# 120 instead of 116 single-row tiles in a two-layer graph convolution: the spacing of the tiles that SyncE and ScalarE fetch row by row

## The chip, the cores and the metric

The kernel runs on one core of a Trainium2 chip. Of the core's engines, TensorE (PE) multiplies, VectorE (DVE) and ScalarE (ACT) work element by element, GpSimd (POOL) issues the gathers with computed row numbers, and SyncE (SP) and ScalarE also issue plain DMAs from queues of their own. The metric is the device time of one execution in microseconds. The median of three runs of the kernel before is 3784.03 us (3783.49 to 3790.35).

## The reference

12500 nodes of 128 features, 200000 edges sorted by destination, 8 relations (edge types). Two layers of the same form run one after the other, then a layer norm. Cut to what matters:

```python
for l in range(2):
    W = einsum('rb,bio->rio', comp[l], basis[l])       # one 128x128 matrix per relation
    xw = einsum('ni,rio->nro', h, W)
    msgs = xw[src, et]                                 # one row per edge: the gather
    summed = segment_sum(msgs, dst * 8 + et)           # per node and relation
    mean = summed / max(count, 1)
    agg = mean.reshape(N, 8, 128).sum(axis=1)
    h = relu(agg + h @ root[l] + bias[l]) + h
out = layernorm(x + h)
```

## The kernel before

The edges lie in 1563 tiles of 128 edges. For each tile the 128 source rows (512 bytes each) must come into SBUF, where a matmul with a one-hot matrix (`dm`, written by VectorE, the weight of each edge in it) sums them by destination. Eight tiles make a quad, 196 quads in all (the last has three tiles); quad q holds tiles 8q to 8q+7.

Layer 1 gathers rows of `x` (12500 rows) and multiplies by the relation matrices after the sum (`means`, `take_means`, `product`, `place`). At its end it writes a table `y_d` of 8 x 12500 rows, each node's features times each relation's matrix. Layer 2 gathers rows of `y_d` and needs only the one-hot matmuls (`add_rows`), a bias, the root matrix and the layer norm (`norm`, in 13 groups of about 1024 nodes).

**How a tile's rows come in.** Nearly all tiles are gathered by GpSimd: `gather(l, q)` issues one indirect DMA of 128 rows for each tile of the quad (line 766) into a ring of seven quad buffers (`rows`), so the gather of quad q+7 needs TensorE to be done with quad q. For the last six quads (190 to 195) the gather of quad q also waits until TensorE is done with quad q-3 (`after = [("done", l)]`). The other tiles are the "single-row" tiles. Lists say which:

```python
# engine, first tile, end, every so many, rows per chunk, quads of lead, host buffers
("SP", 62, 1552, 49, 32, 15, [... 4 hosts in sT ...])
```

Every so many tiles, one tile is left out of GpSimd's work. Its 128 rows are fetched by 128 plain DMAs of one row each, issued by SyncE or ScalarE (`lone_rows`, line 702), in chunks of 32 (16 on ScalarE in layer 1). Ahead of each chunk the engine loads the chunk's row addresses into registers (line 697). A chunk is put into the engine's program 15 quads (10 on ScalarE in layer 1) before the tile's quad, on ScalarE at most one chunk a quad. The rows land in a host buffer that is free at that time, three or four hosts in turn.

**What else is in those queues.** The order of each engine's work is written out once, in program order, by a planner (`Plan`) that adds only the waits that data needs. SyncE also loads `x` for the layer norm (`load_x`) and stores the result. ScalarE has most PSUM evacuations in layer 1. In layer 2 it has, beside its chunks, one square root for each norm group (`root_of`, line 1533); VectorE takes its reciprocal (`one_by`, line 1537) three quads later in program order, ahead of the one-hot matrices of the quads that follow (line 1188). The square root of group n stands at quad 22 + 16n of ScalarE's program, so for n = 10 at quad 182, behind every chunk whose quad of issue comes earlier.

**Between the layers.** GpSimd goes on with quads 0 and 1 of layer 2 while the end of layer 1 is worked off. Before quad 2 it issues one extra gather (line 760) that reads rows which only the last stores of `y_d` bring.

The single-row tiles before: layer 1, SyncE 32 (every 47th from 90), ScalarE 5 and 18 (every 64th); layer 2, SyncE 31 (every 49th from 62), ScalarE 30 (every 50th from 65). 55 + 61 = 116.

Of the kernel before, what the change touches and what calls it, by code (L numbers as in the profile page):

```python
# [8 lines left out]
F32 = mybir.dt.float32  # L9
# [419 lines left out]
def ordered_path(  # L429
# [68 lines left out]
    def keep(shape, dtype, name):  # L498
        return const.tile(shape, dtype, name=name)
# [16 lines left out]
    jmp = keep([P, P], I32, "jmp")  # L516
# [37 lines left out]
    comp_sb = keep([P, L * R * NB], F32, "comp_sb")  # L554
# [84 lines left out]
    def floats(t, n):  # L639
        return t[:, n * P:(n + 1) * P]  # L640

    sT_f = [t.rearrange("p r g k -> p (r g k)") for t in sT_r.tiles]
# [2 lines left out]
    mixer_f = mixer.rearrange("p m k -> p (m k)")  # L645
    idx_f = idx.bitcast(F32)
    lists = [
        [("SP", 90, 1552, 47, 32, 15, [(jmp.bitcast(F32), ["jmp"], []), (comp_sb, ["comp"], []),
                                     (sel.rearrange("p g k -> p (g k)"), ["sel"], [])]),
         ("ACT", 13 * Q + 2, 46 * Q, 8 * Q, 16, 10, [(floats(yr_f, j), yr_cells, yr_cells) for j in range(5)]),  # L650
         ("ACT", 53 * Q + 2, 1552, 8 * Q, 16, 10, [(floats(mixer_f, j), ["mixer"], []) for j in range(2)])],
        [("SP", 62, 1552, 49, 32, 15, [(floats(sT_f[0], j), [("sT", 0, 0), ("sT", 0, 1)], []) for j in range(4)]),
         ("ACT", 65, 1552, 50, 32, 15, [(floats(sT_f[1], j), [("sT", 1, 0), ("sT", 1, 1)], []) for j in range(4)])]]
    single, at_row = [{}, {}], [0, 0]
    for l in range(L):
        for k, (_, t0, t1, by, _, _, hosts) in enumerate(lists[l]):
# [513 lines left out]
    dms, sT, ys, pl, ym = {}, {}, {}, {}, {}  # L1170
# [646 lines left out]
def kernel(  # L1817
# [18 lines left out]
    flag = ctx.enter_context(tc.tile_pool(name="flag", bufs=1))  # L1836
    bad = flag.tile([1, 1], I32, name="bad")
    plan = ordered_path(tc, bad, x, src, dst, et, basis, comp, root, bias, out)
    every = [mybir.EngineType.PE, mybir.EngineType.Activation, mybir.EngineType.DVE, mybir.EngineType.Pool,
             mybir.EngineType.SP]  # L1840
# [36 lines left out]
```

## Time and profile before

| | |
|---|---|
| median of three runs | 3784.03 us |
| the profiled execution's own time | 3783.55 us |
| its span, first to last instruction | 3781.7 us |
| GpSimd busy | 2844.7 us (75%), 3019 instructions |
| TensorE busy | 2413.2 us (64%) |
| VectorE busy | 1694.7 us (45%) |
| ScalarE busy | 354.0 us (9%) |

In the profile, an instruction's row has its start, its duration, the engine, the line, the operation, and in brackets the idle time of the engine before it with what ended it. Issues of DMAs have the engine's name with a q (SPq, ACTq) and count in no busy time: a queue that is full of single-row DMAs reads as idle in the table above. For GpSimd, the 0.3 us between two gathers stand as idle time ended by "issue", which means that nothing seen in the profile was waited for.

### The profile page before, as it was taken

To read this page: it belongs to the slowest core of one execution; us is meant where nothing else is said; L and a number is where in the kernel's file an instruction comes from. 1 tells how busy PE (TensorE), PEld (TensorE's weight loads), DVE (VectorE), ACT (ScalarE), POOL (GpSimd) and SP (SyncE) were. 2 spreads that over 40 slices of the span, in tenths; PEclk is the share of its full clock that TensorE was granted. 3 is DMA by queue.
4 is the path that set the end of the run, shared out by engine and by line. 5 is a ranking of instruction groups with operands and counts; after the bars stand their busy time and mean duration, and the time that the engine had idled before them with its cause. 6 is when DMAs were issued, how large, how long until landed. Compare 5 with 4: busy or idle time off the path is not lost.

```text
span 3781.7 us, 62930 instructions
## 1 busy us (share of the span) xinstructions
PE 2413.2 (64%) x11367; PEld 1933.4 (51%) x11367; DVE 1694.7 (45%) x4752; ACT 354.0 (9%) x794; POOL 2844.7 (75%) x3019
## 2 busy tenths in 40 slices
PE   5777667777666676777765555556566555655655
PEld 3566645555555555665543444444444444444444
DVE  5556424444333333343344444444444444454444
ACT  1121211211111111111100000000000000000000
POOL 7777777777777777777777777777777777777776
PEclk8999879999888888788888787777777777787778
DMA  4122223433322222223232222222222222222222
GB/s 125 56 62 62 56 92 102 123 111 101 99 87 81 89 89 84 84 82 96 92 85 55 56 62 61 65 63 61 66 56 67 66 56 67 60 62 67 67 54 61
DMA packets 155888, 286.71 MB, mean 76 GB/s; under 512 B 67013, under 2 KB 89474, under 8 KB 155482
## 3 DMA queue, kind: packets, MB, share of 16 engines
q0 software_dynamic: 96352, 197.52, 20.3%
q10 hardware_dynamic: 30461, 55.51, 4.5%
q1 hardware_dynamic: 28669, 29.60, 3.0%
q14 instruction: 314, 2.57, 0.2%
q8 instruction: 92, 1.51, 0.2%
HBM read 223.72 MB, written 58.65 MB: 75 GB/s over the span
## 4 chain that ended last, share of the span: by engine, by line
POOL 52%; issue 19%; DMA 11%; PE 9%; ACTq 4%; ACT 2%; DVE 2%; SPq 2%; POOLq 0%; DVEq 0%
POOL rows L766 52%; DMA rows<-y_d,idy 9%; ACTq L702 3%; PE s L1276 2%; PE s L1451 1%; SPq L702 1%; ACT sT L623 1%; ACTq L697 1%; PE y L1308 1%; DVE dm L1188 1%; PE pt L1406 1%; PE ct L959 1%; PE ct L960 1%; DVE arena L949 1%; PE pt L907 1%
## 5 line engine op out<-in xcount | busy, mean ns | idle before, releaser
L766 POOL DMA_INDIRECT rows<-in_x_dram,idx x1508 | 1425.2, 945 | 462.4 <-issue 455.7
L766 POOL DMA_INDIRECT rows<-y_d,idy x1502 | 1417.4, 944 | 458.5 <-issue 446.9
L1188 DVE TENSOR_SCALAR dm<-cols,near,w 128x256 f32<-128x256 f16 x1563 | 723.8, 534 | 952.1 <-PE s L1451 570.3
L1451 PE MATMUL s<-dm,rows 128*128 128x256 f32 x1984 | 659.9, 495 | 447.7 <-DMA rows<-y_d,idy 349.0
L1451 PEld LDWEIGHTS s<-dm,rows 128*128 128x128 f32 x1984 | 491.9, 257 | 580.2 <-issue 316.9
L1188 DVE TENSOR_SCALAR dm<-cols,kr,w 128x128 f32<-128x128 f16 x1563 | 524.9, 400 | 201.8 <-PE s L1276 177.5
L1276 PEld LDWEIGHTS s<-dm,rows 128*128 128x128 f32 x3016 | 436.3, 225 | 291.7 <-DMA rows<-in_x_dram,idx 243.0
L1276 PE MATMUL s<-dm,rows 128*128 128x128 f32 x3016 | 462.1, 313 | 189.0 <-DMA rows<-in_x_dram,idx 182.3
L1451 PE MATMUL ct<-dm,rows 128*128 128x256 f32 x1014 | 341.9, 501 | 294.2 <-DMA rows<-y_d,idy 281.4
L1451 PEld LDWEIGHTS ct<-dm,rows 128*128 128x128 f32 x1014 | 255.3, 262 | 364.2 <-issue 234.5
L1308 PE MATMUL y<-w_sb,sT 128*128 128x128 f32 x1968 | 270.1, 296 | 55.8 <-ACT sT L623 55.8
L1308 PEld LDWEIGHTS y<-w_sb,sT 128*128 128x128 f32 x1968 | 257.0, 211 | 64.6 <-ACT sT L623 63.6
L1406 PE MATMUL pt<-w_sb,arena 128*128 128x512 f32 (+1 forms) x386 | 222.5, 660 | 62.3 <-DVE y_row L626 42.3
L1339 PE MATMUL po<-pl,ys 128*128 128x256 f32 x392 | 138.4, 437 | 140.8 <-ACT sT L623 135.9
L623 ACT ACTIVATE sT<-s 128x512 f32<-128x512 f32 x391 | 213.5, 606 | 83.7 <-PE s L1276 83.4
L626 DVE COPY y_row<-pt 128x512 f32<-128x512 f32 x56 | 38.7, 691 | 364.6 <-PE pt L1406 364.6
L623 ACT ACTIVATE y_row<-pt 128x512 f32<-128x512 f32 (+1 forms) x139 | 83.0, 597 | 1041.7 <-PE s L1276 574.3
L1308 PE MATMUL ct<-w_sb,sT 128*128 128x128 f32 (+1 forms) x1168 | 159.8, 296 | 0.7 <-ACT sT L623 0.7
L1308 PEld LDWEIGHTS ct<-w_sb,sT 128*128 128x128 f32 (+1 forms) x1168 | 155.0, 213 | 1.3 <-ACT sT L623 1.1
L1533 ACT ACTIVATE st<-st,eps 128x8 f32<-128x8 f32 (+1 forms) x13 | 4.0, 308 | 1586.5 <-DMA sT<-y_d 736.9
L1339 PEld LDWEIGHTS po<-pl,ys 128*128 128x128 f32 x392 | 65.2, 201 | 169.0 <-ACT sT L623 159.0
L1360 DVE TENSOR_TENSOR po<-po,carry 128x128 f32<-128x128 f32 x98 | 29.0, 296 | 263.8 <-PE s L1276 242.7
(210 smaller groups left out, 1296.9 us busy)
## 6 DMA issues: line engine op xcount, KB each, us to landing
sT<-y_d SPq DMA_DIRECT2D x3968, 0.5 KB
sT<-y_d ACTq DMA_DIRECT2D x3840, 0.5 KB
y_d<-y_row ACTq DMA_DIRECT2D x96, 512.0 KB
mixer<-in_x_dram ACTq DMA_DIRECT2D x2304, 0.5 KB
rows<-in_x_dram,idx POOLq DMA_INDIRECT x1508
rows<-y_d,idy POOLq DMA_INDIRECT x1502
jmp<-in_x_dram SPq DMA_DIRECT2D x1408, 0.5 KB
comp_sb<-in_x_dram SPq DMA_DIRECT2D x1408, 0.5 KB
```

The source lines that it names most:

```text
L623: act(lambda: nc.scalar.activation(out_t, in_t, AF.Copy), reads, writes)
L626: vec(lambda: nc.vector.tensor_copy(out_t, in_t), reads, writes)
L697: _, at = nc.values_load_multi_w_load_instructions(offs[r:r + 1, l * P + j * ch:l * P + (j + 1) * ch], engines=[mybir.EngineType.SP if e = ...
L702: return [eng.dma_start(o[j * ch + i:j * ch + i + 1, :].bitcast(byte), table_b[bass.ds(v, 4 * D)].rearrange("(p d) -> p d", p=1)) for i, v ...
L766: ins.append(nc.gpsimd.indirect_dma_start(out=t[:, i - q * Q, :], out_offset=None, in_=table_t, in_offset=bass.IndirectOffsetOnAxis(ap=ids ...
L907: last = nc.tensor.matmul(pt[:, b, :], t[:, b, :], m, start=(i == 0), stop=(i == len(parts) - 1))
L1188: emits.append(lambda i=i: nc.vector.tensor_scalar(t[:, i - q * Q, :wide], cols[:, :wide], ids[:, i:i + 1], w[:, i:i + 1], op0=ALU.is_equa ...
L1276: last = nc.tensor.matmul(s_b[i // 4][0][:, i % 4, :], lones[i][0] if i in lones else t[:, i, :], d[:, i, :], start=True, stop=True)
L1308: last = nc.tensor.matmul(y[:m], t[:, r, :nt, :].rearrange("p t k -> p (t k)"), w_sb[:, 0, r, :], start=(r == 0), stop=(r == R - 1))
L1339: ins = nc.tensor.matmul(a, o[:m], t[:m], start=opens, stop=last and not root_in)
L1406: pe(lambda: nc.tensor.matmul(hb[:n].rearrange("p r d -> p (r d)"), hT[:, j * P:j * P + n], w_sb[:, 1, k * H:(k + 1) * H, :].rearrange("p ...
L1451: ins = nc.tensor.matmul(a, lones[i][0] if i in lones else t[:, i, :], d[:, i, :], start=(opens and i == 0), stop=(last and i == n - 1 and ...
```

## The change

```diff
-        [("SP", 90, 1552, 47, 32, 15, [(jmp.bitcast(F32), ["jmp"], []), (comp_sb, ["comp"], []),
+        [("SP", 91, 1552, 45, 32, 15, [(jmp.bitcast(F32), ["jmp"], []), (comp_sb, ["comp"], []),
                                      (sel.rearrange("p g k -> p (g k)"), ["sel"], [])]),
          ("ACT", 13 * Q + 2, 46 * Q, 8 * Q, 16, 10, ...),
          ("ACT", 53 * Q + 2, 1552, 8 * Q, 16, 10, ...)],
-        [("SP", 62, 1552, 49, 32, 15, [(floats(sT_f[0], j), ...) for j in range(4)]),
-         ("ACT", 65, 1552, 50, 32, 15, [(floats(sT_f[1], j), ...) for j in range(4)])]]
+        [("SP", 62, 1552, 47, 32, 15, [(floats(sT_f[0], j), ...) for j in range(4)]),
+         ("ACT", 63, 1552, 48, 32, 15, [(floats(sT_f[1], j), ...) for j in range(4)])]]
```

Three of the five lists get another spacing and two another first tile. Layer 1, SyncE: 33 tiles (91 to 1531) for 32 (90 to 1547). Layer 2, SyncE: 32 tiles (62 to 1519) for 31 (62 to 1532). Layer 2, ScalarE: 32 tiles (63 to 1551) for 30 (65 to 1515). 56 + 64 = 120. GpSimd issues 1 gather fewer in layer 1 and 3 fewer in layer 2; SyncE issues 256 more single-row DMAs and ScalarE 256 more. Every tile still has its one-hot matrix and its matmul; only the buffer that the matmul reads differs. The small loads that bring the row addresses of the tiles carry a few rows more each.

More of the change, by code (lines that the diff above doesn't have):

```diff
@@ L651, in ordered_path @@
          ("ACT", 53 * Q + 2, 1552, 8 * Q, 16, 10, [(floats(mixer_f, j), ["mixer"], []) for j in range(2)])],
-        [("SP", 62, 1552, 49, 32, 15, [(floats(sT_f[0], j), [("sT", 0, 0), ("sT", 0, 1)], []) for j in range(4)]),
-         ("ACT", 65, 1552, 50, 32, 15, [(floats(sT_f[1], j), [("sT", 1, 0), ("sT", 1, 1)], []) for j in range(4)])]]
+        [("SP", 62, 1552, 47, 32, 15, [(floats(sT_f[0], j), [("sT", 0, 0), ("sT", 0, 1)], []) for j in range(4)]),
+         ("ACT", 63, 1552, 48, 32, 15, [(floats(sT_f[1], j), [("sT", 1, 0), ("sT", 1, 1)], []) for j in range(4)])]]
     single, at_row = [{}, {}], [0, 0]
```

## The prediction

> **What bounds the kernel now.** I read the chain that ended last first, then the costliest groups, then GpSimd alone by stretches of time.
>
> ```profile
> span 3781.7 us, 62930 instructions
> POOL 52%; issue 19%; DMA 11%; PE 9%; ACTq 4%; ACT 2%; DVE 2%; SPq 2%; POOLq 0%; DVEq 0%
> L766 POOL DMA_INDIRECT rows<-in_x_dram,idx x1508 | 1425.2, 945 | 462.4 <-issue 455.7
> L766 POOL DMA_INDIRECT rows<-y_d,idy x1502 | 1417.4, 944 | 458.5 <-issue 446.9
> ```
> ```profile
> 2000.00:2100.00 100.00, 75.56 (x81) 0.80 0.25 56
> 2700.00:2800.00 100.00, 75.50 (x81) 0.69 0.27 61
> 3640.00:3740.00 100.00, 75.62 (x81) 0.80 0.20 60
> ```
>
> The second fence is GpSimd's gathers in three stretches of layer 2. A gather costs its busy time and the idle time before it: (1425.2 + 462.4) / 1508 = 1.252 us in layer 1, (1417.4 + 458.5) / 1502 = 1.249 us in layer 2. Nearly all of the idle time ends by "issue", so nothing is waited for; 1508 and 1502 gathers make 1887.6 + 1875.9 = 3763.5 of 3781.7 us. The pace is the same 81 per 100 us whether SyncE and ScalarE send single rows (first two stretches) or have stopped (the third). The kernel is GpSimd's row of gathers, with one real wait in it, between the layers:
>
> ```profile
> 1890.16 0.95 POOL L766 DMA_INDIRECT rows<-y_d,idy  x1 [0.30 <-issue]
> 1908.87 0.94 POOL L766 DMA_INDIRECT rows<-y_d,idy  x1 [0.30 <-issue]
> 1912.13 0.94 POOL L760 DMA_INDIRECT jmp<-y_d,fix_i  x1 [2.31 <-DMA y_d<-y_row]
> ```
> ```profile
> 1866.45 2.46 DMA rows<-in_x_dram,idx
> 1868.95 3.78 PE s L1276 x16
> ...
> 1907.31 4.08 DMA y_d<-y_row
> ```
>
> Layer 2's first 16 gathers run from 1890.16; the 17th (line 760) waits 2.31 us, 2.0 more than the usual 0.30. The chain (second fence) says for what: the rows of quad 192 land at 1868.9, TensorE works from there nearly without a break, and the last store of `y_d` lands at 1911.4.
>
> **The change part by part.** *GpSimd.* One gather less in layer 1, three less in layer 2: 1.25 + 3 x 1.249 = 5.0 us, all on the path, as long as GpSimd never waits.
>
> *The wait between the layers.* Up to quad 192 (tile 1543) the new layer 1 has 33 + 23 = 56 single-row tiles, the old 31 + 23 = 54 (its last, 1547, comes later). So quad 192 lands 2.5 us earlier, but GpSimd comes to line 760 only 1.25 us earlier. If TensorE's work after quad 192 sets the last store, the wait shrinks by 1.25 us; if quad 194, which moves by 1.25 only, sets it, by nothing; if it went altogether, by 2.0. The chain starts at quad 192, but I take the middle, 0.6, and keep 0 and 2.0. Sum: 5.6 us.
>
> *TensorE and VectorE* keep every matmul and one-hot matrix; the buffer read is another. The address loads before layer 1 are as many as before. Nothing there.
>
> *SyncE's queue* gets one tile more in each layer, 128 DMAs and four address loads each. This is hidden only if SyncE keeps up:
>
> ```profile
> 1320.33 50.95 SPq L702 DMA_DIRECT2D jmp<-in_x_dram  x128
> 1374.02 50.38 SPq L702 DMA_DIRECT2D comp_sb<-in_x_dram  x128
> ```
> ```profile
> 2457.40 53.66 SPq L702 DMA_DIRECT2D sT<-y_d  x128
> ...
> 2569.65 108.46 SPq L702 DMA_DIRECT2D sT<-y_d  x256
> 2846.07 0.38 SPq L620 DMA_DIRECT2D out_dram<-x_g  x1
> 2862.44 0.36 SPq L620 DMA_DIRECT2D x_g<-in_x_dram  x1
> ```
>
> Start to start, a tile takes it 53.7 us in layer 1 (1320.33 to 1374.02) and 56.1 in layer 2 (two tiles from 2457.40 to 2569.65). GpSimd takes for 45 tiles of layer 1, less the SyncE one and 45/64 of ScalarE's, 43.3 x 1.252 = 54.2 us, and for 47 tiles of layer 2, less 1 + 47/48, 45.0 x 1.249 = 56.2 us (before: 49 tiles, 58.7). So SyncE goes from some 5% to spare to none, but does not fall behind. If it did, the cover is the ring of seven quads: a quad is 8 x 1.249 = 10.0 us of gathers, and
>
> ```profile
> 2124.41 15.61 DMA rows<-y_d,idy
> ...
> 2141.77 3.82 PE ct L1451 x14
> ```
>
> its rows land 15.6 us after the last issue, and TensorE needs some 5 us more. GpSimd stalls only when TensorE is done six quads, 60 us, late; about 39 us are to spare, for lateness that now grows by 0 to 1 us a tile over 30 tiles. I take nothing.
>
> *ScalarE's queue* gets two tiles more in layer 2, and here the cover is thin. The square roots of the norm stand in the same queue:
>
> ```profile
> 2184.70 0.31 ACT L1533 ACTIVATE st<-st,eps 128x8 f32<-128x8 f32 x1
> 2185.75 154.38 ACTq L702 DMA_DIRECT2D sT<-y_d  x352
> 2340.18 0.31 ACT L1533 ACTIVATE st<-st,eps 128x8 f32<-128x8 f32 x1 [155.17 <-DMA sT<-y_d]
> ...
> 2469.83 156.59 ACTq L702 DMA_DIRECT2D sT<-y_d  x352
> ...
> 2628.78 141.90 ACTq L702 DMA_DIRECT2D sT<-y_d  x320
> ...
> 2773.06 150.01 ACTq L702 DMA_DIRECT2D sT<-y_d  x352
> ...
> 2925.59 120.85 ACTq L702 DMA_DIRECT2D sT<-y_d  x288
> 3056.73 0.31 ACT L1533 ACTIVATE st<-st,eps 128x8 f32<-128x8 f32 x1 [133.31 <-DVE dm L1188]
> ...
> 3211.08 137.95 ACTq L702 DMA_DIRECT2D sT<-y_d  x320
> 3360.08 0.31 ACT L1533 ACTIVATE st<-st,eps 128x8 f32<-128x8 f32 x1 [150.99 <-DVE dm L1188]
> 3362.38 130.62 ACTq L702 DMA_DIRECT2D sT<-y_d  x320
> 3520.32 0.31 ACT L1533 ACTIVATE st<-st,eps 128x8 f32<-128x8 f32 x1 [159.94 <-DVE dm L1188]
> 3522.62 102.46 ACTq L702 DMA_DIRECT2D sT<-y_d  x256
> ```
> ```profile
> 2185.04 0.21 DVE L1537 RECIPROCAL st<-st 128x8 f32<-128x8 f32 x1 [15.35 <-ACT st L1533]
> 2340.52 0.20 DVE L1537 RECIPROCAL st<-st 128x8 f32<-128x8 f32 x1 [24.78 <-ACT st L1533]
> 2340.80 3.70 DVE L1188 TENSOR_SCALAR dm<-cols,near,w 128x256 f32<-128x256 f16 x8
> ```
>
> Each row of ScalarE's is a run of chunks of 32. At the first two square roots ScalarE is late, and VectorE stands 15.35 and 24.78 us before the reciprocal, with the next one-hot matrices behind it. Later ScalarE is early and itself idle before the root: 10.3 us (3046.4 to 3056.7), 11.1 and 27.3, all by its rows' ends. With the 50 spacing GpSimd needs (50 - 1 - 50/49) x 1.249 = 59.9 us a tile, with 48 it needs 57.4. ScalarE's own pace is 14.45 us a chunk at its slowest (2469.83 to 2628.78, 11 chunks), 14.25 and 13.9 in neighbours (from 2185.75; from 2773.06, where SyncE stood still from 2846 to 2862): 57.8 to 55.5 a tile. So it no longer gains on GpSimd, and VectorE will wait at nearly every root. A wait of 25 to 35 us delays TensorE by perhaps 10 to 25, inside the 39 us. I take nothing in mid-layer.
>
> **The place where the cover ends** is the tail, where a gather needs TensorE only three quads back. Root 10 stands at quad 182, behind all 128 chunks (120 before); behind it come the reciprocal, the matrices of quad 188, TensorE's quad 188, and on that waits the gather of quad 191:
>
> ```profile
> 3726.91 0.95 POOL L766 DMA_INDIRECT rows<-y_d,idy  x1 [0.30 <-issue]
> ```
> ```profile
> 3709.55 5.38 PE L1451 MATMUL s<-dm,rows 128*128 128x256 f32 x16 [4.36 <-DMA rows<-y_d,idy]
> ```
>
> That gather should start at 3726.9 - 5.6 = 3721.3, so root 10 may come at 3721.3 - 5.4 (matmuls) - 3.7 (matrices) - 0.5 = 3711.7 at the latest. Before, chunk 20 ended at the first root, 2184.7, and chunk 120 at 3522.62 + 102.46 = 3625.1; less 48.7 us of idling, 13.9 us a chunk. From 2182.7 (2 us earlier), 108 chunks end at 3684 at that pace, at 3743 at the slowest, 14.45. The first half of the layer, where both queues run full, is nearer to the second; the stops of SyncE for its `x` loads bring it back. I take 14.1: 3706, 6 us before the limit, no stall. Bounds: 0 and 3743 - 3712 = 31 us.
>
> Here a page of the Trainium skill speaks against the change: "DMA: Bandwidth & Descriptors", in "Issuing engines are not separate DMA queues", says that DMAs from the SP, ACT and GpSimd queues all end on the same 16 DMA engines and interleave, so that spreading them saves only the time to issue. Taken alone it would give no gain, 3784, were the transfers the bound; the unchanged 81 gathers per 100 us say that issue is the bound, but the 15.61 us that rows take with both queues full, against 3.31 at the end, agree that the queues share something.
>
> ```profile
> 3764.36 3.31 DMA rows<-y_d,idy
> ```
>
> **The forecast.** The profiled execution took 3783.55 us, 0.5 under the median. 3783.55 - 5.6 = 3777.95; against the median, 3784.03 - 5.6 = 3778.4 us. About 0.2%, 7.6 us, is what a measurement of this kernel can tell from no change, so this is a small true gain that reads as none.
>
> **The rivals.** *ScalarE late at root 10* (slower). It decides from 14.16 us a chunk on: (3711.7 - 2182.7) / 108. At 14.21 the gain is used up, from 14.28 it is over 0.2% slower, at 14.45 the time is 3778.4 + 31 = 3809. For it: that pace was seen, and the density keeps both queues full. Against it: the whole-layer mean of 13.9, and that SyncE, done earlier, leaves ScalarE alone. *SyncE late*: should a layer 2 tile take it 58 us, it loses 1.8 x 31 = 56 us, 17 more than the ring covers: 3795. Against it: 56.1 was measured with ScalarE's queue full. *Nothing gained*, the transfers being the bound: 3784; the three equal stretches speak against it. *More gained*: the wait of 2.0 us goes entirely, 3777.0.
>
> **How the numbers follow.** Forecast with its bounds 0.58, its own range 3776.5 to 3779.5; 0.08 of it may read beyond 0.2% by scatter (the runs shown lie 0.5 apart at best). ScalarE late by under 13 us, 0.14; late by more, 0.21 (3792 to 3809); SyncE late, 0.05; nothing gained, 0.02. Faster 0.08; same 0.50 + 0.14 + 0.02 = 0.66; slower 0.26. The range, 3776.5 to 3797, leaves out 0.08 below and some 0.1 above.
>
> **What would show it.** 1507 and 1499 gathers at 1.25 us; the wait at line 760 between 0.3 and 2.3; at line 1537 waits on ScalarE of 10 to 35 us at most of the norm groups, ScalarE without idle time before its roots; GpSimd idle 0.3 before every gather. A row of GpSimd near 3720 with more idle before it, and a root 10 after 3712, would be the rival. The forecast is wrong if ScalarE's chunks take over 14.2 us, or if the ring's 39 us are less than I reckon.

## The result, and the profile after

The median of 22 runs is 3777.84 us (3775.18 to 3781.36), that of 22 runs of the kernel before 3783.03 us (3781.28 to 3790.35). The ratio is 0.9987, with a 95% interval of 0.9981 to 0.9993: 5.2 us or 0.13% less time, clear of the noise of so many runs and inside the 0.2% that the prediction had set as its bound for "same". The predicted time was 3778.4 us. The profiled execution took 3777.95 us with a span of 3776.2 us, 5.5 under the span before.

GpSimd is still the kernel. These rows of the gathers are of the kernel after (count; shortest, median and longest in ns; first and last start in us):

```profile
L766 POOL DMA_INDIRECT rows<-in_x_dram,idx x1507: 940/944/1235, 4.7 to 1887.7; - x189
L766 POOL DMA_INDIRECT rows<-y_d,idy x1499: 940/944/997, 1888.9 to 3763.7; - x188
```

and these of the kernel before:

```profile
L766 POOL DMA_INDIRECT rows<-in_x_dram,idx x1508: 940/944/1177, 4.6 to 1888.9; - x189
L766 POOL DMA_INDIRECT rows<-y_d,idy x1502: 940/944/1009, 1890.2 to 3768.1; - x188
```

In the kernel after, only two gathers of all waited for more than the usual 0.30 us (apart from the very first), the one between the layers and one in the tail:

```profile
1909.69 0.94 POOL L760 DMA_INDIRECT jmp<-y_d,fix_i  x1 [1.09 <-issue]
3712.53 0.94 POOL L766 DMA_INDIRECT rows<-y_d,idy  x1 [1.99 <-PE s L1451]
```

These times add up to the change of the span. Four gathers at 1.25 us are 5.0 us. The wait at line 760 is 1.09 us where it was 2.31, 1.2 less. The tail has a new wait of 1.99 us, 1.7 over the usual. So the last gather starts 4.4 us earlier (3763.7 for 3768.1; the first one was 0.1 later). After it the end takes 12.5 us (3776.2 less 3763.7) where it took 13.6. Together 5.5 us. Why the end is shorter is not shown; the two other profiled kernels with these lists in which GpSimd sets the time have 12.6 and 12.7 us.

The new wait in the tail is what the prediction did not have. The chain that ended last shows it:

```profile
3690.86 15.65 DMA rows<-y_d,idy
3706.65 0.67 PE s L1451 x2
3707.54 4.72 PE s L1451 x14
3712.53 0.94 POOL rows L766
```

The last gather of quad 187 is issued at 3690.86 and its rows land 15.65 us later. TensorE starts at once and takes about 5.6 us, and the first gather of quad 190, which must wait for TensorE three quads back, starts right behind. By GpSimd's own pace it would have started 16 gathers after that last one, at 3690.86 + 16 x 1.249 = 3710.8. In the kernel before, both queues were done with their rows by 3634 us, and TensorE began with the same quad's rows 2.6 us after its last gather:

```profile
3696.95 0.95 POOL L766 DMA_INDIRECT rows<-y_d,idy  x1 [0.30 <-issue]
```
```profile
3699.59 1.08 PE L1451 MATMUL s<-dm,rows 128*128 128x256 f32 x2 [4.73 <-DMA rows<-y_d,idy]
```

ScalarE's queue, with its roots, now looks like this (a run of chunks, then the root behind it):

```profile
2195.92 154.42 ACTq L702 DMA_DIRECT2D sT<-y_d  x352
2350.39 0.31 ACT L1533 ACTIVATE st<-st,eps 128x8 f32<-128x8 f32 x1 [155.20 <-DMA sT<-y_d]
...
3410.49 0.31 ACT L1533 ACTIVATE st<-st,eps 128x8 f32<-128x8 f32 x1 [153.26 <-DMA sT<-y_d]
...
3550.74 154.52 ACTq L702 DMA_DIRECT2D sT<-y_d  x352
3705.32 0.31 ACT L1533 ACTIVATE st<-st,eps 128x8 f32<-128x8 f32 x1 [156.72 <-DMA sT<-y_d]
```

Every root up to the one at 3705.32, root 10, stands directly behind ScalarE's own chunks; the idle time of 10 to 27 us that ScalarE had before roots is gone. VectorE pays for it at line 1537, in all norm groups together (second row: us, times) and, as examples, at groups 1, 9 and 10:

```profile
L1537 DVE RECIPROCAL st<-st x13: 168/206/207, 2195.2 to 3769.7; 128x8 f32<-128x8 f32 x12, 106x2 f32<-106x2 f32 x1
  ACT st L1533: 255.9, 13
```
```profile
2350.73 0.21 DVE L1537 RECIPROCAL st<-st 128x8 f32<-128x8 f32 x1 [34.21 <-ACT st L1533]
3548.62 0.20 DVE L1537 RECIPROCAL st<-st 128x8 f32<-128x8 f32 x1 [3.54 <-ACT st L1533]
3705.66 0.21 DVE L1537 RECIPROCAL st<-st 128x8 f32<-128x8 f32 x1 [6.85 <-ACT st L1533]
```

Before it was two long waits, 15.35 and 24.78 us. None of the new ones reaches GpSimd in mid-layer.

### The profile page after: what moved, and what is told of

Read it like the earlier page. It is cut to its first block, busy times and chain, and to the rows that moved or that the text cites. A ratio compares the mean times of both kernels' runs of the same rounds, so it can differ in the third digit from the quotient of the medians.

```text
span 3776.2 us, 63981 instructions
## 1 busy us (share of the span) xinstructions
PE 2383.8 (63%) x11367; PEld 1910.0 (51%) x11367; DVE 1692.4 (45%) x4752; ACT 354.0 (9%) x794; POOL 2840.9 (75%) x3015
## 4 chain that ended last, share of the span: by engine, by line
POOL 53%; issue 19%; DMA 12%; PE 8%; ACTq 4%; DVE 2%; ACT 2%; POOLq 0%; DVEq 0%; SPq 0%
POOL rows L766 53%; DMA rows<-y_d,idy 11%; ACTq L702 3%; PE s L1276 2%; ACTq L697 1%; PE y L1308 1%; ACT sT L623 1%; DVE dm L1188 1%; PE ct L959 1%; PE ct L960 1%; PE s L1451 1%; DMA rows<-in_x_dram,idx 1%; DVE arena L949 1%; PE pt L907 1%; PE ct L1451 0%
## 5 line engine op out<-in xcount | busy, mean ns | idle before, releaser
L1451 PE MATMUL s<-dm,rows 128*128 128x256 f32 x1984 | 625.7, 477 | 464.1 <-DMA rows<-y_d,idy 318.1
L1451 PEld LDWEIGHTS s<-dm,rows 128*128 128x128 f32 x1984 | 471.9, 247 | 587.0 <-issue 330.3
L1276 PEld LDWEIGHTS s<-dm,rows 128*128 128x128 f32 x3014 | 434.2, 224 | 280.2 <-DMA rows<-in_x_dram,idx 228.1
```

Source lines behind the costliest of these rows:

```text
L1276: last = nc.tensor.matmul(s_b[i // 4][0][:, i % 4, :], lones[i][0] if i in lones else t[:, i, :], d[:, i, :], start=True, stop=True)
L1451: ins = nc.tensor.matmul(a, lones[i][0] if i in lones else t[:, i, :], d[:, i, :], start=(opens and i == 0), stop=(last and i == n - 1 and ...
```

## The experiments

The kernels of this section ran on six chips. On three of them the kernel before takes about 3782 us, as in the result. On the other three it takes 5877 to 5889 us, and there SyncE's queue, not GpSimd, sets the time; those runs are told last.

### The late wait taken out

Theory: the 1.99 us at 3712.5, and more of the same in other runs, is the wait of the last six quads' gathers for TensorE three quads back, and TensorE is late because rows land some 15 us after issue while ScalarE's queue still runs. Rival: root 10, behind all of ScalarE's chunks, is what is late. First the wait itself was taken out of layer 2 of the kernel after; the ring of seven quads still holds the gathers back where data needs it. (The expectation of no_late_wait, to which this one points, stands in the last part of this section.)

```diff
-        after = [("done", l)] if q >= NQ - LATE else []
+        after = [("done", l)] if l == 0 and q >= NQ - LATE else []
```

> The same kernel as in the run no_late_wait, once more. If the issue of single rows takes SyncE 51 us a tile, as in the profiles of before and after, the expectation of that run holds: 1.5 to 3 us under the kernel after, so 0.18 to 0.22% under the kernel before, and no wait of GpSimd near 3712. If it takes 60 to 87 us a tile, as in the first four runs, SyncE bounds the whole kernel and the 120 tiles make it some 2% slower than 116.

Measured: 3776.14 us (3775.7 to 3777.04), beside 3782.41 of the kernel before on that chip, ratio 0.9983 (0.9974 to 0.9992). Its gathers wait nowhere. The spread is 1.3 us where the kernel after has 6.2. The gain over the kernel before is 6.3 us instead of 5.2, a difference of medians that is not clear of the noise, since the intervals of the two kernels overlap. What the wait costs is read from the two profiled executions: the spans are 3773.9 and 3776.2 us, and between them lie the wait in the tail (1.7 over the usual) and the wait at line 760 (0.8 more than the 0.30 here), less 0.2 by which the ends and beginnings differ. That the wider spread of the kernel after is the wait's is not shown: the kernel before, whose profile has no wait in its tail, spreads by 5.1 us on this chip (3780.11 to 3785.17). The end after the last gather did not grow:

```profile
L766 POOL DMA_INDIRECT rows<-y_d,idy x1499: 940/944/1022, 1888.9 to 3761.3; - x188
```

With a span of 3773.9 us that is 12.6 us, for 12.5. This kernel has the lowest median of those run.

### Late rows or a late root

The kernel after once more, with the late wait, but without the square root and the epsilon in the norm (which changes the result): VectorE no longer waits for ScalarE at all.

```diff
-nc.vector.reciprocal(st[:p, :k, A + M], st[:p, :k, A + M]), [sc + (2,)], [sc + (3,)])
+nc.vector.reciprocal(st[:p, :k, A + M], st[:p, :k, A + 1]), [sc + (1,)], [sc + (3,)])
...
-todo.extend([turn, add, stats, aggr, root_of, lambda: None, lambda: None, one_by, scale, store])
+todo.extend([turn, add, stats, aggr, lambda: None, lambda: None, lambda: None, one_by, scale, store])
```

> As for no_scalar_root (the square root and the epsilon left out of the norm), on a chip where SyncE takes 51 us a tile: if late rows hold the tail, a wait of 1 to 4 us near 3712 stays and the time is 3776 to 3779; if root 10 holds it, the wait goes and the time is 3776.1, within 1 us. Where SyncE takes 60 to 87 us a tile the time is some 6017 us again, and nothing is told of the tail.

Measured: 3777.17 us (3775.34 to 3781.81), ratio 0.9988 (0.9979 to 0.9997), the time and the spread of the kernel after. The wait in the tail is still there, and so is the chain to it:

```profile
3716.09 0.94 POOL L766 DMA_INDIRECT rows<-y_d,idy  x1 [1.71 <-PE s L1451]
```
```profile
3694.70 15.62 DMA rows<-y_d,idy
3710.45 1.19 PE s L1451 x2
3711.64 0.43 PE s L1454 x2
3712.07 3.77 PE s L1451 x14
3716.09 0.94 POOL rows L766
```

So it is the rows and not the root. The same run shows that the 256 us of VectorE's waits were worth nothing: they are gone, and the time is the same within the noise.

The profiled execution is the slowest of this run's, 3781.81 us, but not through longer waits: 1.37 us at line 760 and 1.71 in the tail are 3.08 together, as 1.09 and 1.99 are in the kernel after. What is longer is the row of gathers:

```profile
L766 POOL DMA_INDIRECT rows<-in_x_dram,idx x1507: 940/945/1160, 4.9 to 1889.9; - x189
L766 POOL DMA_INDIRECT rows<-y_d,idy x1499: 940/945/1030, 1891.2 to 3767.3; - x188
```

From the first to the last gather layer 1 takes 1885.0 us for 1883.0 in the kernel after, and layer 2 takes 1876.1 for 1874.8. So 3.3 of the 3.8 us by which this span (3780.0 us) is longer are a slightly slower pace of the gathers, so that a part of the spread between runs can be that pace.

### 32 gathers more

The kernel without the late wait, with SyncE's two lists and ScalarE's list of layer 2 at every 70th tile:

```diff
-("SP", 91, 1552, 45,   ("SP", 62, 1552, 47,   ("ACT", 63, 1552, 48,
+("SP", 91, 1552, 70,   ("SP", 62, 1552, 70,   ("ACT", 63, 1552, 70,
```

> Without the late wait, and three lists every 70th tile: 21 tiles of SyncE's in layer 1 for 33, 22 for 32 in layer 2 by SyncE and by ScalarE, so 32 gathers more than in the kernel without the late wait. On a chip where SyncE takes 51 us a tile GpSimd's row sets the time: 3776.1 + 32 x 1.249 = 3816 us, 1% slower than 120 tiles. On one where it takes 60 to 87 us a tile, SyncE's 43 tiles at up to 92 us need 3956 us where its 65 needed 5980, so the time falls from about 6017 to between 3900 and 4300 us; if it stays above 5500 there, it is not the single rows that bound it.

Measured: 3816.50 us (3814.26 to 3817.32), ratio 1.009 (1.0074 to 1.0105). That is 40.4 us over the kernel without the late wait, 1.26 us for each of the 32 gathers, where 1.249 was reckoned. A single-row tile is worth what its gather costs, as long as the queues keep up.

### SyncE past its pace

Again without the late wait, and SyncE's list of layer 2 every 45th: two tiles more, and more than its queue can do.

```diff
-         [("SP", 62, 1552, 47, 32, 15,
+         [("SP", 62, 1552, 45, 32, 15,
```

> Without the late wait, and SyncE's list of layer 2 every 45th (34 tiles for 32), two gathers less. GpSimd needs (45 - 1 - 45/48) x 1.249 = 53.8 us a tile, SyncE takes 56.1: 2.3 x 33 = 76 us behind at the end, some 30 to 40 more than the ring covers. By this rule (the rival SyncE late) the time is 3776.1 - 2.5 + 30 to 40 = 3804 to 3814, with GpSimd waiting for TensorE and TensorE for sT in the last third of layer 2. If SyncE's pace is not what it seemed, or a late tile holds nothing up, 3773.6.

> As for sp_45, on a chip where SyncE takes 51 us a tile in layer 1: SyncE late by some 76 us at the end of layer 2, 30 to 40 more than the ring covers, 3804 to 3814 us, or 3773.6 if its pace or the cover is better than reckoned. On a chip like the last one it is 6083 us again.

Measured in sp_45_b, on a chip of the first kind (sp_45 stands in the table further down): 3821.47 us (3820.36 to 3824.02), ratio 1.0104 (1.0087 to 1.012). The rival was right in kind and 7 to 17 us short in size. In this order: the chain's shares by engine, three waits of GpSimd, two waits of TensorE for single-row tiles, SyncE's last tile, and GpSimd's gathers:

```profile
SPq 35%; POOL 26%; issue 17%; PE 7%; ACTq 6%; DMA 4%; ACT 3%; DVE 2%; POOLq 0%; DVEq 0%
```
```profile
3157.42 0.94 POOL L766 DMA_INDIRECT rows<-y_d,idy  x1 [3.39 <-PE ct L1451]
...
3324.53 0.94 POOL L766 DMA_INDIRECT rows<-y_d,idy  x1 [5.01 <-PE s L1451]
...
3501.99 0.94 POOL L766 DMA_INDIRECT rows<-y_d,idy  x1 [15.39 <-PE s L1451]
```
```profile
3495.65 1.19 PE L1451 MATMUL s<-dm,rows 128*128 128x256 f32 x2 [41.29 <-DMA sT<-y_d]
...
3799.53 1.19 PE L1451 MATMUL s<-dm,rows 128*128 128x256 f32 x2 [18.59 <-DMA sT<-y_d]
```
```profile
3749.82 48.61 SPq L702 DMA_DIRECT2D sT<-y_d  x128
```
```profile
L766 POOL DMA_INDIRECT rows<-y_d,idy x1497: 940/944/1023, 1888.9 to 3781.9; - x188
```

The three waits cost 23 us. The last gather starts at 3781.9, but SyncE's last tile is issued until 3798.4, and the end comes 37.5 us after the last gather instead of 12.6, 25 us more. 3776.1 - 2.5 + 23 + 25 = 3821.6. What the expectation had wrong is the cover: it took 30 to 40 us of ring off SyncE's lateness, but at the end of the layer no ring is left to cover anything, and the time is SyncE's own: 34 tiles from 1911 to 3798, 55.5 us each, and 21 us of work behind them. At every 47th, its 32 tiles are done at 3694, some 67 us before the last gather; two more tiles of 55.5 us do not fit in.

### The chips on which SyncE sets the time

On three chips the same kernels gave other times. Kernels on one chip share the runs of the kernel before.

> Layer 1's SyncE list alone is changed (33 tiles for 32), layer 2 as before. If the wait at line 760 follows layer 1's end, it falls from 2.31 us to about 1.1, as in the kernel after, and with the gather saved (1.25) the time is 2.5 us under the kernel before. Rival: the 1.09 us of the kernel after was scatter or came from layer 2's first tiles; then the wait stays near 2.3 and the time falls by 1.25 alone. In the tail no wait of GpSimd, as before.

> Layer 2's SyncE list alone is changed (32 tiles for 31). The sum gives 1.25 us less than before. ScalarE's list is the old one, so the root of group 10 should stay near 3625 to 3640 us and GpSimd should have no wait near 3712. Rival (SyncE does not keep up at 47): a row of GpSimd with idle time before it, ended by SyncE's sT, and a time over the kernel before.

> Layer 2's ScalarE list alone is changed (32 tiles for 30, every 48th, from 61 where the kernel after has 63, since 63 would meet a SyncE tile here). The sum gives 2.5 us less than before. Theory (rows land late): ScalarE's queue runs to about 3700 us, rows then still land some 15 us after issue, and a gather of the last six quads waits 0 to 3 us for TensorE, so that 0 to 2.5 us of gain are left. Rival (the root of group 10 is what is late): it comes after 3708 and the matrices of VectorE behind it, not the rows, are what TensorE waits for ahead of that gather.

> The kernel after, but in layer 2 the gathers of the last six quads do not wait until TensorE is done three quads back; only the ring of seven quads holds them. Theory: the 1.99 us before the gather at 3712.5 and the spread of the kernel after (3775 to 3781 us) are that wait; both go, and the time is 1.5 to 3 us under the kernel after, 3775 to 3776. Rival: the wait covers something else, such as rows of the last quads that land later when more gathers are out at once; then the end after the last gather grows by what the wait gives back, and the time stays near 3777.8.

> The kernel after, but the norm leaves out the square root and the epsilon (VectorE takes the reciprocal of the variance itself), so that VectorE never waits for ScalarE's queue; its output is not the reference's. Theory (rows land late in the tail): a gather of quad 190 still waits 1 to 4 us near 3712, ended by TensorE, and the time is that of the kernel after, 3776 to 3779, with the same spread. Rival (root 10 is what is late): the wait goes and the time is that of the kernel without the late wait, 3776.1, with a spread of about 1 us. Either way the 256 us that VectorE waited at line 1537 go, and if they go without a change of time in mid-layer, the ring had covered them.

> As for l1_only, where SyncE takes 51 us a tile: layer 1's SyncE list alone is changed. One gather less, 1.25 us; the wait at line 760 between 0.3 and 2.3 us (it was 2.31 before, 1.09 after, 0.30 without the late wait). If the denser layer 1 shortens that wait, the time is 2.5 us or more under the kernel before; if the wait only scatters, 1.25 us under it. No wait of GpSimd in the tail.

> Without the late wait, and SyncE's lists denser still: every 44th in layer 1 (34 tiles for 33) and every 46th in layer 2 (33 for 32), two gathers less. Layer 1 has the margin: in the kernel after SyncE's tiles landed 25 to 46 us before GpSimd's end of their quad. In layer 2 GpSimd needs (46 - 1 - 46/48) x 1.249 = 55.0 us a tile, SyncE takes 56.1, so it falls behind by some 1.1 x 32 = 35 us, which the ring covers by about 30 to 39. If the cover holds: 3776.1 - 2.5 = 3773.6. If not, a wait of GpSimd for TensorE late in layer 2 of up to 15 us.

The edits of those not shown above, each against the kernel before, or (the last) against the kernel without the late wait:

```diff
l1_only    -("SP", 90, 1552, 47,   +("SP", 91, 1552, 45,
l2_sp      -("SP", 62, 1552, 49,   +("SP", 62, 1552, 47,
l2_act     -("ACT", 65, 1552, 50,  +("ACT", 61, 1552, 48,
two_denser -("SP", 91, 1552, 45,   +("SP", 91, 1552, 44,
           -("SP", 62, 1552, 47,   +("SP", 62, 1552, 46,
```

| chip, before | kernel | tiles by SyncE | us | ratio (95%) |
|---|---|---|---|---|
| 1, 5889.48 | l2_act | 63, as before | 5883.40 | 0.9989 (0.9965 to 1.0014) |
| 1 | l2_sp | 64 | 5939.59 | 1.0079 (1.0053 to 1.0104) |
| 1 | l1_only | 64 | 5957.96 | 1.0103 (1.0078 to 1.0127) |
| 1 | no_late_wait | 65 | 6016.95 | 1.0202 (1.0177 to 1.0228) |
| 2, 5877.39 | l1_only_b | 64 | 5951.27 | 1.0126 (1.0102 to 1.0149) |
| 2 | no_scalar_root | 65 | 6016.51 | 1.0235 (1.0214 to 1.0257) |
| 3, 5877.92 | sp_45 | 67 | 6083.25 | 1.0362 (1.0341 to 1.0383) |
| 3 | two_denser | 67 | 6096.38 | 1.0387 (1.0371 to 1.0403) |

Every tile given to SyncE costs 50 to 74 us there, and tiles given to ScalarE cost nothing that the noise lets us see. The chain of no_late_wait on chip 1, and SyncE's chunks in it:

```profile
SPq 59%; issue 36%; another core or an unknown queue 2%; PE 1%; DVE 1%; DMA 0%; ACT 0%; ACTq 0%; DVEq 0%; POOLq 0%
```
```profile
3002.45 397.49 SPq L702 DMA_DIRECT2D sT<-y_d  x528
```

528 DMAs in 397.5 us are 0.75 us each. On the chip of no_late_wait_b the same program has

```profile
2000.07 226.22 SPq L702 DMA_DIRECT2D sT<-y_d  x542
```

0.42 us each. None of the expectations above could be answered there. The four that asked for the parts of the change alone, and two_denser, stay open: the change was not measured in parts where GpSimd is the bound.

## Why the prediction was right, step by step

*Gathers.* 1507 and 1499 at 1.25 us, all on the path: as the sum had it, and every_70 gives 1.26 us for one gather from times alone.

*The wait between the layers.* Taken as 0.6 us of gain, between 0 and 2.0; it was 1.2 in the two profiled executions. That this follows from the denser layer 1 is not shown. Three more traces with the same layer 1 have 0.30, 1.37 and 0.52 us at that place, and every_70, whose layer 1 is sparser than before, has 0.30. So it scatters by more than the term, and the kernel meant to settle it ran where SyncE was the bound.

*SyncE.* That it just keeps up at every 47th was right. In the kernel after its layer 2 runs from 1911.2 to 3694.1, 32 tiles at 55.7 us (56.1 had been read), against the 56.2 us that GpSimd needs. The rival SyncE late is real two tiles further on, and it is what bounds the kernel on the slower chips.

```profile
L702 SPq DMA_DIRECT2D sT<-y_d x4096: 224/228/614, 1911.2 to 3694.1; - x196
```

*ScalarE's queue and the norm.* VectorE waits at the roots as foretold, 3.5 to 34.2 us at ten of them and 6.85 at root 10, and the ring covers them; no_scalar_root_b shows that they cost nothing. Root 10 came at 3705.32, where 3706 was worked out from 14.1 us a chunk. The pace was that: the first root, at 2194.9, stands behind 21 chunks now (672 DMAs of 32 a chunk) and not 20, so that 107 lie between it and root 10, and (3705.3 - 2194.9) / 107 = 14.1. The rival ScalarE late at root 10 stayed away, by the prediction's own limit of 3711.7 by 6.4 us.

*The place where the cover ends.* This step named the right place, the gathers that wait for TensorE three quads back, but followed only one of the two things that TensorE needs. It asked when the matrices of quad 188 would come, behind root 10, and took the rows as there. It used the 15.61 us that rows take with both queues full for the ring of seven quads only. With three quads there is no room for it: 15.65 us for the rows and 6.0 us from there to the start of the waiting gather are 21.7, against 16 gathers of 1.249, 20.0. So instead of "no stall" the tail loses 1.7 us in the profiled execution. The Trainium skill's rule in "DMA: Bandwidth & Descriptors", "Issuing engines are not separate DMA queues", that all queues end on the same engines, was weighed only as a bound on the whole. The trace agrees with it at one late place, where gathered rows take 15.65 us beside the single rows and about 3 us without them; that the shared engines are the reason is not shown.

*The sum.* 5.6 us were forecast and 5.2 measured. Two terms that were not forecast, 1.7 lost in the tail and 1.1 gained after the last gather, lie on both sides, and the wait between the layers is larger by 0.6. The size is right partly because small errors cancelled.

## What to carry to other kernels

When an engine that merely issues sets the pace, price a change by its instructions, and then look for the places where the usual slack is smaller than elsewhere: here three quads instead of seven. At such a place add up everything that the waiting work needs (rows, matrices, matmuls), not only what the change makes later. Work moved onto another queue costs no issue time until that queue's own total reaches the end of the row, though its transfers can make other rows late, as in the tail here; past that point its whole time counts, and no ring helps at the end.

## What the runs showed of the hardware that was not expected

Rows gathered by GpSimd land 15.6 us after issue while SyncE and ScalarE both send single rows, and within about 3 us once they have stopped (in the kernel after, TensorE starts at 3724.56 on quad 190's rows, whose last gather was issued at 3721.25). The mean busy share of the DMA engines is low in both cases. Two stretches of the kernel after (length, GpSimd's busy time and gathers, clock, DMA share, GB/s):

```profile
3640.00:3690.00 50.00, 37.77 (x41) 0.77 0.30 61
3720.00:3750.00 30.00, 22.68 (x25) 0.81 0.21 56
```

The share is 0.30 with the single rows and 0.21 without. The semaphore events in the traces tell more. The landing of a gather is counted there in sixteen steps, 112 for the seven gathers of quad 187. Of these 112, 105 had come 2.6 us after the last gather was issued; the other seven, one for each gather, came one after another from 3698.97 to 3706.51. So not all of a gather's rows are late, but one of sixteen shares, and TensorE waits for it. A mean over 16 engines hides that: by an estimate from the two rows above, the difference of 0.09 is the whole time of 1.4 engines of the 16. For quads 190 to 193 all steps come within 4 us of the last issue. In sp_45_b, where SyncE alone sends single rows from 3706 to 3798, no step is late any more in quads issued from 3722 on, so one such queue is not enough. Why that one share waits is not shown by these runs.

Chips differ in how steadily they issue DMAs. These rows are of no_late_wait on chip 1 (shortest, median and longest in ns):

```profile
L702 SPq MOVE sT<-y_d x4096: 2/29/1470, 2933.5 to 5988.9; - x196
L702 SPq DMA_DIRECT2D sT<-y_d x4096: 2/228/1437, 2933.5 to 5989.0; - x196
```

and these of the same program in no_late_wait_b:

```profile
L702 SPq MOVE sT<-y_d x4096: 29/29/29, 1910.2 to 3698.0; - x196
L702 SPq DMA_DIRECT2D sT<-y_d x4096: 224/228/566, 1910.3 to 3698.1; - x196
```

The medians agree, but on chip 1 an instruction that only moves a register, 29 ns (at most 38) in all traces of the faster chips, now and then takes up to 1470 ns. GpSimd's gathers take 945 ns on the mean there and 944 here. The cause is open. What follows is that the margin of 0.5 us a tile, on which this change lives, belongs to the chip as much as to the kernel: on two of the three slower chips these lists were run (in no_late_wait and no_scalar_root), and there they made it 2.0 and 2.4% slower than the kernel before.
